# Windowed attention in layer 0: bias coefficients of 16 rows a head in 128x64 tiles, and the one-hot products in one turn

## The chip, the cores and the metric

The kernel runs on one core of a Trainium2 chip. The metric is the time of one execution on the device in microseconds (us), the median of several runs. A core has TensorE (PE in the profile; its weight loads are shown apart as PEld), VectorE (DVE), ScalarE (ACT), GpSimd (POOL) and SyncE (SP), which issues the transfers here. Matmul results land in PSUM[...]; VectorE and ScalarE carry them from there to SBUF.

## The reference

The input x is fp32, 2 images of 128 channels and 256x256 pixels. Two layers follow each other, both of the form x + f(groupnorm(x)). Layer 1 is a pair of convolutions whose product is added; the change doesn't touch it. Layer 0 is windowed attention with 4 heads of 32 channels: windows of 8x8 queries look at 12x12 keys around them.

```python
qkv = jnp.einsum('bchw,oc->bohw', x, W_qkv)
...
q = q * SCALE
attn = jnp.einsum('bnd,bmd->bnm', q, k)
attn = attn + rel_pos_emb(q, rel_height, rel_width) + FIXED_MASK
attn = jax.nn.softmax(attn, axis=-1)
out = jnp.einsum('bnm,bmd->bnd', attn, v)
...
return jnp.einsum('bchw,oc->bohw', out, W_out)
```

FIXED_MASK is minus infinity wherever the row distance or the column distance of query and key has the wrong parity. A query therefore meets only 6 key rows and 6 key columns, and a window falls into four classes by row parity and column parity, of 16 queries and 36 keys each. rel_pos_emb adds to each score one number for the key's column and one for its row; both are inner products of the query with a small table. For a query and a head there are thus 6 column coefficients and 6 row coefficients, from which the biases of all its keys are put together.

## The kernel before

An image is cut into 32 strips of 8 rows (strip k of 64 over both images). A strip is worked off in two units, u = 2k + r, one for each row parity r; both column parities c are handled inside the unit. Windows are taken in pairs side by side (e is 0 or 1), 16 pairs to a strip; the 8 pairs of one half of the strip share a PSUM bank for scores. A pair uses 60 keys in common, 10 columns j by 6 rows i, padded to 64; window e may see columns 4e to 4e + 5 only.

The scores of a unit stand in four banks, `sc[g][half]`: g is a pair of heads, half a half of the strip; column parity c picks partitions 0 to 63 or 64 to 127. Everything else that TensorE writes goes through one pool of four banks, `ps_pj`, handed out in turn: a new tile gets the bank of the fourth last, and must wait until that one has been read.

The biases are made in two steps:

- `coefficients(k, t2)` (L341). A query's place within its class is given by t2 (column, 0 to 3) and t1 (row, 0 to 3). For each of the 16 places, a matmul of the weights `wb[:, t2, t1]` (4 heads of 32 rows) with the gathered inputs `xq[:, t2, t1]` (4 classes a times 32 windows m, 128 columns) gives the coefficients of all queries in that place. The 32 rows of a head hold 6 column coefficients for window 0, the same 6 again for window 1, 6 row coefficients and 2 rows for flags. ScalarE (L358) writes the even windows into the tile `cf`, VectorE (L361) the odd ones; a scale and an addend of each row, `keep`, zero the rows of the other window and set a flag to 1.
- `biases(u, turn)` (L385). A matmul with a fixed one-hot matrix `hot` (32 rows by 64 keys for a head) spreads the coefficients over the keys, straight into the score banks; the flag rows bring the large negative number for keys that a window mustn't see. A turn is 8 matmuls of 32x64 with 256 columns. Turn 0 begins the banks, turn 1 fills in the other head of each pair; then `scores(u)` (L401) adds the products of keys and queries.

`by_place(k, columns)` (L292) gathers the normalised input into `xq` on GpSimd, two of the four t2 in each unit, for the strip after.

The order is written by hand for every engine (`manual_schedule`), so each engine runs its instructions in the order of the main loop (L493 to L526). In a unit u = 2k + r TensorE does: turn 1 of the biases, scores (L408), values (`f_pv`, L374), coefficients of the next strip for two t2 (`f_pa`, L352), attention outputs (`f_o`, L433), turn 0 of the biases of unit u + 1 (L393), its queries (`f_pq`, L330) and keys (`f_pk`, L309), and the output projection of u (`f_py`, L466). ScalarE takes exponentials (L417), half of the value copies (L380), coefficients, queries (L334) and keys (L310). VectorE takes the other value copies, coefficients, the division by the softmax sum (L439, L440), a transpose (L451), statistics (L111), the residual sum (L467) and the normalisation (L285).

Of the kernel before, what the change touches and what calls it, by code (L numbers as in the profile page):

```python
# [19 lines left out]
P = 128  # L20
# [28 lines left out]
def host_constants():  # L49
    ident = np.eye(P, dtype=np.float32)  # L50
    gavg = np.zeros((P, P), np.float32)
    for g in range(P // 4):
        gavg[4 * g : 4 * g + 4, 4 * g : 4 * g + 4] = 0.25

    kb = np.zeros((HEADS, 32, 6, 10), np.float32)
    for c in range(10):
        kb[:, c, :, c] = 1.0
    for r in range(6):
        kb[:, 10 + r, r, :] = 1.0
    kb[:, 16, :, 6:] = NEG  # L60
    kb[:, 17, :, :4] = NEG
    flag = np.zeros((2, 4 * NPAIR * 4, 2, 4), np.float32)
    flag[0, :, 0] = 1.0
    flag[1, :, 1] = 1.0


    hot = np.zeros((HEADS, 32, 64), np.float32)
    for key in range(64):
        j, i = divmod(key, 6)
        if key < 60:  # L70
            if j < 6:
                hot[:, j, key] = 1.0
            if j >= 4:
                hot[:, 6 + j - 4, key] = 1.0
            hot[:, 12 + i, key] = 1.0
        hot[:, 18, key] = 0.0 if j < 6 else NEG
        hot[:, 19, key] = 0.0 if 4 <= j < 10 else NEG

    keep = np.zeros((HEADS, 32, 2, 2), np.float32)
    for e in range(2):  # L80
        keep[:, 6 * e : 6 * e + 6, e, 0] = 1.0
        keep[:, 12:18, e, 0] = 1.0
        keep[:, 18 + e, e, 1] = 1.0

    sel = np.zeros((4, 32, P), np.float32)
    for ch in range(P):
        sel[:, ch % 8, ch] = 1.0
    return {
        "c_ident": ident,
        "c_sel": sel.reshape(P, P),  # L90
        "c_gavg": gavg,
        "c_kb": kb.reshape(P, 60),
        "c_flag": flag.reshape(2, 4 * NPAIR, 32),
        "c_hot": hot.reshape(P, 64),
        "c_keep": keep.reshape(P, 4),
        "c_head": np.stack([(np.arange(P) // DH % 2 == i) for i in range(2)], 1).astype(np.float32),
    }
# [47 lines left out]
def attention_fast(tc, io, x1_d, norm, st_x, st_y, tags, ends):  # L145
# [6 lines left out]
    with ExitStack() as l0:  # L152
# [8 lines left out]

        wqkvT = cload("wqkvT", io["w_qkvT"], [P, 3 * P])
        woT = cload("woT", io["w_outT"], [P, P])
        hot = cload("hot", io["c_hot"], [P, 64])
        keep = cload("keep", io["c_keep"], [P, 4])
        head = cload("head", io["c_head"], [P, 2])
        wq_s = cst.tile([P, P], F32, tag="f_wq_s", name="f_wq_s")
# [14 lines left out]
            for g in range(2)  # L182
        ]

        xq = cst.tile([P, 4, 4, 4, 2 * NPAIR], F32, tag="f_xq", name="f_xq")
        wb = cst.tile([P, 4, 4, HEADS, 32], F32, tag="f_wb", name="f_wb")
        for i in range(2):
            nc.gpsimd.memset(xn[i], 0.0)
            for r in range(2):
# [6 lines left out]
        with ExitStack() as setup:  # L196
            sp = setup.enter_context(tc.tile_pool(name="f_setup", bufs=6))


            wq_nat = sp.tile([P, P], F32, tag="wq_nat", name="f_wq_nat", bufs=1)  # L200
            nc.sync.dma_start(wq_nat, io["w_q"])
            relT = sp.tile([P, 2 * NREL], F32, tag="relT", name="f_relT", bufs=1)
            nc.sync.dma_start(relT, io["relT"])
            g_rel = sp.tile([P, HEADS, 2 * NREL], F32, tag="g_rel", name="f_g_rel", bufs=1)
            for h in range(HEADS):
                pg = ps_pj.tile([P, 512], F32, tag="pj", name=f"f_pg_{h}")


                for o in (0, NREL):
                    for m in (0, 64):  # L210
                        nc.tensor.matmul(
                            pg[m : m + 64, o : o + NREL], wq_nat[32 * h : 32 * h + 32, m : m + 64],
                            relT[32 * h : 32 * h + 32, o : o + NREL], start=True, stop=True,
                        )
                nc.scalar.mul(g_rel[:, h, :], pg[:, : 2 * NREL], SCALE)
            for t in range(4):
                o = 11 - 2 * t
                nc.scalar.copy(wb[:, t, 0, :, 0:6], g_rel[:, :, o : o + 11 : 2])
                nc.scalar.copy(wb[:, t, 0, :, 6:12], g_rel[:, :, o : o + 11 : 2])
                for t1 in range(1, 4):  # L220
                    nc.scalar.copy(wb[:, t, t1, :, 0:12], wb[:, t, 0, :, 0:12])
                o = NREL + 11 - 2 * t
                for t2 in range(4):
                    nc.scalar.copy(wb[:, t2, t, :, 12:18], g_rel[:, :, o : o + 11 : 2])
            for s in range(NS):
                t = sp.tile([P, 8, W], F32, tag="sx", name=f"f_sx_0_{s}")
                nc.sync.dma_start(t, x[0, :, 8 * s : 8 * s + 8, :])
                norm.chunk(st_x[0], 4 * s, t)
# [63 lines left out]
        def by_place(k, columns):  # L292
            cells = xn[k % 2].rearrange("p r c j i -> p (r c) j i")[:, :, 1:129, 1:5]
            for t2 in columns:
                nc.gpsimd.tensor_copy(xq[:, t2], cells.rearrange("p a (m b) i -> p b i a m", b=4)[:, t2])  # L295

        def old_keys(u):
            k, r = divmod(u, 2)
# [39 lines left out]

            return [lambda c=c: part(c) for c in range(2)]

        def coefficients(k, t2):  # L341

            if t2 == 0:
                cfs[k] = wk.tile([P, 4, NPAIR, 2, 4, 4], F32, tag="cf", name=f"f_cf_{k}")
            cf = cfs[k].rearrange("p a n e b t -> p e b t (a n)")
            bank = []

            def part(t1):
                if t1 == 0:
                    bank.append(ps_pj.tile([P, 512], F32, tag="pj", name=f"f_pa_{k}_{t2}"))  # L350
                pa = bank[0]
                nc.tensor.matmul(  # L352
                    pa[:, P * t1 : P * t1 + P], wb[:, t2, t1].rearrange("p h x -> p (h x)"),
                    xq[:, t2, t1].rearrange("p a m -> p (a m)"), start=True, stop=True,
                )
                if t1 == 3:
                    by_e = pa.rearrange("p (t m e) -> p e t m", t=4, e=2)
                    nc.scalar.activation(  # L358
                        cf[:, 0, t2], by_e[:, 0], AF.Identity, bias=keep[:, 1:2], scale=keep[:, 0:1]
                    )  # L360
                    nc.vector.tensor_scalar(  # L361
                        cf[:, 1, t2], by_e[:, 1], keep[:, 2:3], keep[:, 3:4], ALU.mult, ALU.add
                    )

            return [lambda t=t: part(t) for t in range(4)]

        def values(u, j):
            k, r = divmod(u, 2)
# [13 lines left out]
                    pv[rows].rearrange("p (n h d) -> p n h d", n=4, h=HEADS),  # L382
                )

        def biases(u, turn):  # L385

            k, r = divmod(u, 2)
            for i in range(2):
                half = (i + turn) % 2
                for h in (i, i + 2):  # L390
                    rows = slice(32 * h, 32 * h + 32)
                    for c in range(2):
                        nc.tensor.matmul(  # L393
                            sc[h // 2][half][64 * c : 64 * c + 64, :, i], hot[rows, :],
                            cfs[k][rows, 2 * r + c, 8 * half : 8 * half + 8].rearrange(
                                "p n e b t -> p n (e b t)"
                            ),
                            start=turn == 0, stop=False, skip_group_check=True,
                        )

        def scores(u):  # L401
            k, r = divmod(u, 2)
# [83 lines left out]
        with tc.manual_schedule(engines=ORDERED):  # L486
            normalise(0)
            by_place(0, range(4))
            for t2 in range(4):
                emit(coefficients(0, t2))  # L490
            biases(0, 0)
            emit(queries(0) + keys(0))
            for u in range(NU):  # L493
                k, r = divmod(u, 2)
                b, s = divmod(k, NS)
                later, more = u + 1 < NU, k + 1 < NB * NS
                if r == 0:
                    if k + 2 < NB * NS:
                        load_rows(k + 2)
                    if more:  # L500
                        normalise(k + 1)
                if u in stats_at:
                    input_stats(u)
                if more:
                    by_place(k + 1, (2 * r, 2 * r + 1))
                if later:
                    old_keys(u + 1)
                biases(u, 1)
                scores(u)
                for j in range(4):  # L510
                    values(u, j)
                if more:
                    emit(coefficients(k + 1, 2 * r) + coefficients(k + 1, 2 * r + 1))
                attend(u)
                turn(u)
                if later:

                    biases(u + 1, 0)
                    emit(queries(u + 1) + keys(u + 1))
                if u > 0:  # L520
                    result_stats(u - 1)
                project(u)
                if u in stats_at:
                    load_next()
                del qs[u]
# [819 lines left out]
```

## Time and profile before

| | |
|---|---|
| median of 3 runs | 3400.35 us (3399.28 to 3402.16) |
| span of the profiled run | 3402.5 us |
| layer 0, first to last coefficient matmul | 101.0 to 2182.8 us |
| granted TensorE clock | 0.991 |
| TensorE busy, 500 to 1000 us | 500.00 us |
| VectorE busy in it | 389.82 us |
| ScalarE busy in it | 288.05 us |
| GpSimd busy in it | 117.12 us |
| data moved | 104 GB/s over the span |

The groups of instructions that the change touches, with the count of records (a matmul leaves two), their busy time and the mean of one:

| line, engine | what | records | busy us | mean ns |
|---|---|---|---|---|
| L352 PE | coefficients, 128x128 with 128 columns | 2048 | 268.5 | 286 |
| L393 PE | one-hot products, 32x64 with 256 columns | 4096 | 176.4 | 400 |
| L358 ACT | coefficients to `cf`, 128x256 | 256 | 209.8 | 819 |
| L361 DVE | coefficients to `cf`, 128x256 | 256 | 196.0 | 765 |
| L295 POOL | gather into `xq`, 128x512 | 256 | 346.9 | 1386 |

Busy time of TensorE is a union: matmuls overlap, so a mean of 286 ns for a record says nothing of the rate. The rate is read from the chain or from a timeline, as the length of a stretch divided by its matmuls. A busy share alone doesn't say what sets the time either; for that one looks at which engine the chain of work lies on, and at whether that engine ever waits.

### The profile page before, as it was taken

To read this page: it belongs to the slowest core of one execution; us is meant where nothing else is said; L and a number is where in the kernel's file an instruction comes from. 1 tells how busy PE (TensorE), PEld (TensorE's weight loads), DVE (VectorE), ACT (ScalarE), POOL (GpSimd) and SP (SyncE) were. 2 spreads that over 40 slices of the span, in tenths; PEclk is the share of its full clock that TensorE was granted. 3 is DMA by queue.
4 is the path that set the end of the run, shared out by engine and by line. 5 is a ranking of instruction groups with operands and counts; after the bars stand their busy time and mean duration, and the time that the engine had idled before them with its cause. 6 is when DMAs were issued, how large, how long until landed. Compare 5 with 4: busy or idle time off the path is not lost.

```text
span 3402.5 us, 116586 instructions
## 1 busy us (share of the span) xinstructions
PE 3248.6 (95%) x52814; PEld 1977.8 (58%) x52814; DVE 2632.3 (77%) x3955; ACT 1602.4 (47%) x2675; POOL 940.0 (28%) x598
## 2 busy tenths in 40 slices
PE   0799999999999999999999999989999999999997
PEld 0567777777777777777777777733333333333333
DVE  8667777777777777767777676678888888888887
ACT  0455555555555555555555555523333323333332
POOL 2212122222222212122122221123333333333333
PEclk9999999999999999999999999989999999999999
DMA  9223233232332212222122221133333332333332
GB/s 397 104 102 117 90 123 114 93 117 97 116 117 86 92 65 80 71 81 80 65 80 79 73 80 65 53 103 124 122 112 113 124 124 99 121 112 114 124 124 83
DMA packets 115896, 360.28 MB, mean 106 GB/s; under 512 B 8128, under 2 KB 74304, under 8 KB 90816
## 3 DMA queue, kind: packets, MB, share of 16 engines
q1 hardware_dynamic: 115392, 352.72, 29.2%
q8 instruction: 419, 6.86, 0.8%
q14 instruction: 85, 0.70, 0.1%
HBM read 218.48 MB, written 134.22 MB: 104 GB/s over the span
## 4 chain that ended last, share of the span: by engine, by line
PE 95%; issue 2%; DVE 1%; DMA 1%; POOL 1%; ACT 0%; SPq 0%; POOLq 0%; DVEq 0%
PE a_p L636 26%; PE f_pv L374 14%; PE f_pa L352 8%; PE f_s L408 8%; PE f_o L433 7%; PE f_pq L330 7%; PE f_pk L309 7%; PE f_py L466 7%; PE g L622 5%; PE f_s L393 5%; PE b L706 2%; DMA f_sx<-in_x 0%; DVE t L695 0%; DMA raw<-f_x 0%; POOL f_kt L190 0%
## 5 line engine op out<-in xcount | busy, mean ns | idle before, releaser
L380 DVE COPY f_vt<-f_pv 64x512 f32<-64x512 f32 x512 | 355.0, 695 | 314.0 <-ACT f_vt L380 313.8
L636 PE MATMUL a_p<-xm,w 128*128 128x512 f32 (+1 forms) x1288 | 581.5, 597 | 0.0
L295 POOL COPY f_xq<-f_xn 128x512 f32<-128x512 f32 x256 | 346.9, 1386 | 846.2 <-DVE f_xn L285 846.2
L334 ACT ACTIVATE f_q<-f_pq,f_head 128x512 f32<-128x512 f32 x512 | 310.0, 688 | 362.0 <-PE f_pq L330 362.0
L374 PE MATMUL f_pv<-f_wqkvT,f_xn 128*64 128x128 f32 x8192 | 476.1, 274 | 0.0
L374 PEld LDWEIGHTS f_pv<-f_wqkvT,f_xn 128*64 128x64 f32 x8192 | 445.2, 137 | 8.7
L688 ACT ACTIVATE t<-t,w 128x1024 f32<-128x1024 f32 x128 | 147.3, 1151 | 619.9 <-DVE t L683 619.9
L636 PEld LDWEIGHTS a_p<-xm,w 128*128 128x128 f32 x1288 | 238.3, 189 | 331.4 <-issue 331.1
L695 DVE SCALAR_TENSOR_TENSOR t<-t,w,t 128x1024 f32<-128x1024 f32 x256 | 420.2, 1641 | 6.8 <-ACT t L688 1.7
L417 ACT ACTIVATE f_p<-f_s 128x512 f32<-128x512 f32 x512 | 264.3, 603 | 340.0 <-PE f_s L408 339.9
L380 ACT COPY f_vt<-f_pv 64x512 f32<-64x512 f32 x512 | 298.4, 583 | 111.7 <-PE f_pv L374 111.3
L723 POOL TENSOR_TENSOR y<-y,raw 128x768 f32<-128x768 f32 x62 | 169.2, 2729 | 541.5 <-DVE y L715 493.4
L724 POOL TENSOR_TENSOR y<-y,raw 128x1280 f32<-128x1280 f32 x64 | 246.3, 3848 | 164.3 <-DVE y L715 164.3
L278 POOL COPY f_xn<-f_xn 128x1048 f32<-128x1048 f32 x62 | 71.2, 1148 | 796.9 <-PE f_pv L374 796.9
L352 PE MATMUL f_pa<-f_xq,f_wb 128*128 128x128 f32 x2048 | 268.5, 286 | 17.1 <-DVE f_vt L380 11.2
L408 PEld LDWEIGHTS f_s<-f_q,f_kt 64*64 64x64 f32 x16384 | 252.2, 135 | 49.6 <-issue 49.6
L361 DVE TENSOR_SCALAR f_cf<-f_pa,f_keep 128x256 f32<-128x256 f32 x256 | 196.0, 765 | 100.3 <-ACT f_cf L358 100.2
L408 PE MATMUL f_s<-f_q,f_kt 64*64 64x64 f32 x16384 | 269.9, 220 | 0.0
L467 DVE TENSOR_TENSOR f_x<-f_py,f_raw 128x512 f32<-128x512 f32 x256 | 177.0, 692 | 119.7 <-PE f_py L466 119.7
L352 PEld LDWEIGHTS f_pa<-f_xq,f_wb 128*128 128x128 f32 x2048 | 244.2, 195 | 38.8 <-issue 25.7
L433 PE MATMUL f_o<-f_vt,f_p 128*32 128x66 f32 x16384 | 263.4, 222 | 0.0
L330 PE MATMUL f_pq<-f_xn,f_wq_s 128*128 128x512 f32 x512 | 255.4, 619 | 0.0
(117 smaller groups left out, 4458.8 us busy)
## 6 DMA issues: line engine op xcount, KB each, us to landing
f_raw<-in_x SPq DMA_DIRECT2D x62, 1280.0 KB, 8.1
f_sx<-in_x SPq DMA_DIRECT2D x64, 1024.0 KB, 7.7
f_x<-f_x SPq DMA_DIRECT2D x128, 512.0 KB, 3.4
out<-y SPq DMA_DIRECT2D x64, 1024.0 KB, 4.9
raw<-f_x SPq DMA_DIRECT2D x64, 640.0 KB, 6.4
raw<-f_x SPq DMA_DIRECT2D x62, 384.0 KB, 6.9
f_raw<-in_x SPq DMA_DIRECT2D x2, 1024.0 KB, 8.0
raw_pre<-f_x SPq DMA_DIRECT2D x2, 384.0 KB, 5.2
```

What stands on the lines that cost most here:

```text
L295: nc.gpsimd.tensor_copy(xq[:, t2], cells.rearrange("p a (m b) i -> p b i a m", b=4)[:, t2])
L330: nc.tensor.matmul(pq, wq_s, xn[k % 2][:, r, c, 1:129, 1:5], start=True, stop=True)
L334: nc.scalar.activation(q[:, c, :, i], pq.rearrange("p (n x) -> p n x", n=NPAIR), AF.Copy, scale=head[:, i : i + 1],)
L352: nc.tensor.matmul(pa[:, P * t1 : P * t1 + P], wb[:, t2, t1].rearrange("p h x -> p (h x)"), xq[:, t2, t1].rearrange("p a m -> p (a m)"), s ...
L374: nc.tensor.matmul(pv[64 * c : 64 * c + 64, P * n : P * n + P], xt[:, r, c, o : o + 64], wvT, start=True, stop=True,)
L380: (nc.vector.tensor_copy if c else nc.scalar.copy)(vt[rows, 4 * j : 4 * j + 4, :, c, 0:32], pv[rows].rearrange("p (n h d) -> p n h d", n=4 ...
L408: nc.tensor.matmul(sc[g][n // 8][64 * c : 64 * c + 64, n % 8].rearrange("p i x -> p (i x)"), keys_k[rows, c, 48 * n : 48 * n + 64], qs[u][ ...
L417: nc.scalar.activation(pts[u][:, g, 8 * half : 8 * half + 8].rearrange("p n i x -> p (n i x)"), sc[g][half].rearrange("p n i x -> p (n i x ...
L433: nc.tensor.matmul(po[32 * h : 32 * h + 32, n - lo], p[:, h // 2, n, h % 2], vt[:, n, h], start=True, stop=True,)
L636: nc.tensor.matmul(pa[:, : n * W], w, rows, start=i == 0, stop=i == len(terms) - 1)
L695: nc.vector.scalar_tensor_tensor(t3[:, j : j + 4], t1[:, j + tap : j + tap + 4, :], w3[:, tap : tap + 1], t3[:, j : j + 4], ALU.mult, ALU.add,
L724: nc.gpsimd.tensor_tensor(y[:, 3:8, :], y[:, 3:8, :], raws[b, s][:, 0:5, :], ALU.add)
```

## The change

Half of the rows in a coefficient matmul carried a second copy of the column coefficients, flags of the other window, or nothing. The change gives a head 16 rows: 6 column coefficients, 6 row coefficients, one flag, 3 unused. The weights of a place are then 128x64, and the two halves of a strip are computed beside each other in two column tiles of the array, 64 columns each: half 0 lands in partitions 0 to 63, half 1 in 64 to 127. One call makes the coefficients of two t2 into a single bank, and one ScalarE and one VectorE operation of 512 elements a partition empty it. What they tell apart is no longer the window e but the head i of a pair: each writes all columns and `keep` zeroes the rows of the other head.

The window is now told apart by the one-hot matrix, of which there are two (`hot[rows, e]`), with the flag's negative number in the columns that the window mustn't see. A block of 32 rows holds the two heads of a pair in one half, so the 16 one-hot products of a unit are still 16 matmuls of 32x64 with 256 columns. All are issued in one turn, right before the scores.

GpSimd's gathers are split by half: four of 256 elements a unit in place of two of 512. In the setup, the weights `wb` are laid out by other copies.

```diff
-    hot = np.zeros((HEADS, 32, 64), np.float32)
+    hot = np.zeros((2, HEADS, 16, 2, 64), np.float32)
...
+    keep = np.zeros((2, HEADS, 16, 2, 2), np.float32)
+    for i in range(2):
+        keep[:, i::2, 0:12, i, 0] = 1.0
+        keep[:, i::2, 12, i, 1] = 1.0
...
-        xq = cst.tile([P, 4, 4, 4, 2 * NPAIR], F32, tag="f_xq", name="f_xq")
-        wb = cst.tile([P, 4, 4, HEADS, 32], F32, tag="f_wb", name="f_wb")
+        xq = cst.tile([P, 4, 2, 4, 4, NPAIR], F32, tag="f_xq", name="f_xq")
+        wb = cst.tile([P, 4, 4, HEADS, 16], F32, tag="f_wb", name="f_wb")
...
             for t2 in columns:
-                nc.gpsimd.tensor_copy(xq[:, t2], cells.rearrange("p a (m b) i -> p b i a m", b=4)[:, t2])
+                for half in range(2):
+                    nc.gpsimd.tensor_copy(
+                        xq[:, t2, half],
+                        cells[:, :, 64 * half : 64 * half + 64].rearrange(
+                            "p a (m b) i -> p b i a m", b=4
+                        )[:, t2],
+                    )
...
-        def coefficients(k, t2):
...
+        def coefficients(k, r):
...
+            if r == 0:
+                cfs[k] = wk.tile([P, 2, 4, 8, 2, 16], F32, tag="cf", name=f"f_cf_{k}")
+            pa = ps_pj.tile([P, 512], F32, tag="pj", name=f"f_pa_{k}_{r}")
+            for t in range(8):
+                t2, t1 = 2 * r + t // 4, t % 4
+                for half in range(2):
+                    nc.tensor.matmul(
+                        pa[64 * half : 64 * half + 64, 64 * t : 64 * t + 64],
+                        wb[:, t2, t1].rearrange("p h x -> p (h x)"),
+                        xq[:, t2, half, t1].rearrange("p a m -> p (a m)"), start=True, stop=True,
+                    )
+            src = pa.rearrange("p (t m e) -> p e m t", t=8, e=2)
+            for i in range(2):
+                dst = cfs[k][:, :, :, :, i, 8 * r : 8 * r + 8].rearrange("p e a n t -> p e (a n) t")
+                if i == 0:
                     nc.scalar.activation(
-                        cf[:, 0, t2], by_e[:, 0], AF.Identity, bias=keep[:, 1:2], scale=keep[:, 0:1]
-                    )
+                        dst, src, AF.Identity, bias=keep[:, 1:2], scale=keep[:, 0:1]
+                    )
+                else:
                     nc.vector.tensor_scalar(
-                        cf[:, 1, t2], by_e[:, 1], keep[:, 2:3], keep[:, 3:4], ALU.mult, ALU.add
-                    )
+                        dst, src, keep[:, 2:3], keep[:, 3:4], ALU.mult, ALU.add
+                    )
...
-        def biases(u, turn):
+        def biases(u):
...
+            for e in range(2):
+                for half in range(2):
+                    for g in range(2):
+                        rows = slice(64 * half + 32 * g, 64 * half + 32 * g + 32)
+                        for c in range(2):
+                            nc.tensor.matmul(
+                                sc[g][half][64 * c : 64 * c + 64, :, :, 16 * e : 16 * e + 16].rearrange(
+                                    "p n i x -> p (n i) x"
+                                ),
+                                hot[rows, e],
+                                cfs[k][rows, e, 2 * r + c].rearrange("p n i x -> p (n i x)"),
+                                start=e == 0, stop=False, skip_group_check=True,
+                            )
...
-                biases(u, 1)
+                biases(u)
                 scores(u)
...
-                    emit(coefficients(k + 1, 2 * r) + coefficients(k + 1, 2 * r + 1))
+                    coefficients(k + 1, r)
                 attend(u)
                 turn(u)
                 if later:
-
-                    biases(u + 1, 0)
                     emit(queries(u + 1) + keys(u + 1))
```

More of the change, by code (lines that the diff above doesn't have):

```diff
@@ L64, in host_constants @@
     flag[1, :, 1] = 1.0
-    hot = np.zeros((HEADS, 32, 64), np.float32)
+    hot = np.zeros((2, HEADS, 16, 2, 64), np.float32)
     for key in range(64):
         j, i = divmod(key, 6)
[L70 to L83, printed above, removed]
+        for e in range(2):
+            if 0 <= j - 4 * e < 6:
+                hot[:, :, j - 4 * e, e, key] = 1.0
+            else:
+                hot[:, :, 12, e, key] = NEG
+            if key < 60:
+                hot[:, :, 6 + i, e, key] = 1.0
+    keep = np.zeros((2, HEADS, 16, 2, 2), np.float32)
+    for i in range(2):
+        keep[:, i::2, 0:12, i, 0] = 1.0
+        keep[:, i::2, 12, i, 1] = 1.0
     sel = np.zeros((4, 32, P), np.float32)
@@ L93, in host_constants @@
         "c_flag": flag.reshape(2, 4 * NPAIR, 32),
-        "c_hot": hot.reshape(P, 64),
+        "c_hot": hot.reshape(P, 128),
         "c_keep": keep.reshape(P, 4),
@@ L163, in attention_fast @@
         woT = cload("woT", io["w_outT"], [P, P])
-        hot = cload("hot", io["c_hot"], [P, 64])
+        hot = cload("hot", io["c_hot"], [P, 2, 64])
         keep = cload("keep", io["c_keep"], [P, 4])
@@ L217, in attention_fast @@
                 o = 11 - 2 * t
[L218 to L221, printed above, removed]
+                for t1 in range(4):
+                    nc.scalar.copy(wb[:, t, t1, :, 0:6], g_rel[:, :, o : o + 11 : 2])
                 o = NREL + 11 - 2 * t
                 for t2 in range(4):
-                    nc.scalar.copy(wb[:, t2, t, :, 12:18], g_rel[:, :, o : o + 11 : 2])
+                    nc.scalar.copy(wb[:, t2, t, :, 6:12], g_rel[:, :, o : o + 11 : 2])
             for s in range(NS):
@@ L339, in queries @@
             return [lambda c=c: part(c) for c in range(2)]
-        def coefficients(k, t2):
[L343 to L354, printed above, removed]
-                )
-                if t1 == 3:
-                    by_e = pa.rearrange("p (t m e) -> p e t m", t=4, e=2)
+        def coefficients(k, r):
[14 more added lines that the diff above has]
+                if i == 0:
                     nc.scalar.activation(
-                        cf[:, 0, t2], by_e[:, 0], AF.Identity, bias=keep[:, 1:2], scale=keep[:, 0:1]
+                        dst, src, AF.Identity, bias=keep[:, 1:2], scale=keep[:, 0:1]
                     )
+                else:
                     nc.vector.tensor_scalar(
-                        cf[:, 1, t2], by_e[:, 1], keep[:, 2:3], keep[:, 3:4], ALU.mult, ALU.add
+                        dst, src, keep[:, 2:3], keep[:, 3:4], ALU.mult, ALU.add
                     )
-            return [lambda t=t: part(t) for t in range(4)]
         def values(u, j):
@@ L383, in values @@
                 )
-        def biases(u, turn):
+        def biases(u):
             k, r = divmod(u, 2)
[L388 to L398, printed above, removed]
-                        )
+            for e in range(2):
+                for half in range(2):
[10 more added lines that the diff above has]
+                            )
         def scores(u):
@@ L488, in attention_fast @@
             by_place(0, range(4))
-            for t2 in range(4):
-                emit(coefficients(0, t2))
-            biases(0, 0)
+            coefficients(0, 0)
+            coefficients(0, 1)
             emit(queries(0) + keys(0))
```

## The prediction

> **What bounds the kernel now.** I read first the busy shares, then the chain of work that ended last.
>
> ```profile
> PE 3248.6 (95%) x52814; PEld 1977.8 (58%) x52814; DVE 2632.3 (77%) x3955; ACT 1602.4 (47%) x2675; POOL 940.0 (28%) x598
> ...
> PE 95%; issue 2%; DVE 1%; DMA 1%; POOL 1%; ACT 0%; SPq 0%; POOLq 0%; DVEq 0%
> ```
>
> TensorE is busy 95% of the span, and the chain lies on it for the same 95%: what it no longer has to do comes off the span, until another engine holds it up. The same chain in order of time, from 1000 to 1040 us, shows one unit of layer 0 (start, length, what; x counts records, two to a matmul):
>
> ```profile
> 1009.44 2.02 PE f_s L408 x128
> 1011.47 3.65 PE f_pv L374 x64
> 1015.11 1.98 PE f_pa L352 x16
> 1017.10 1.98 PE f_o L433 x128
> 1019.07 0.62 PE f_s L393 x16
> 1019.69 1.92 PE f_pq L330 x4
> 1021.61 1.75 PE f_pk L309 x4
> 1023.36 1.72 PE f_py L466 x4
> 1025.07 0.62 PE f_s L393 x16
> 1025.69 2.02 PE f_s L408 x128
> ```
>
> No gap: a unit is 2.02 + 3.65 + 1.98 + 1.98 + 0.62 + 1.92 + 1.75 + 1.72 + 0.62 = 16.26 us, and there are 128. The change touches 1.98 (coefficients) and 2 x 0.62 (one-hot products). What the other engines do with the coefficients is in the groups:
>
> ```profile
> L334 ACT ACTIVATE f_q<-f_pq,f_head 128x512 f32<-128x512 f32 x512 | 310.0, 688 | 362.0 <-PE f_pq L330 362.0
> L358 ACT ACTIVATE f_cf<-f_pa,f_keep 128x256 f32<-128x256 f32 x256 | 209.8, 819 | 91.8 <-PE f_pa L352 80.1
> L361 DVE TENSOR_SCALAR f_cf<-f_pa,f_keep 128x256 f32<-128x256 f32 x256 | 196.0, 765 | 100.3 <-ACT f_cf L358 100.2
> L467 DVE TENSOR_TENSOR f_x<-f_py,f_raw 128x512 f32<-128x512 f32 x256 | 177.0, 692 | 119.7 <-PE f_py L466 119.7
> ```
>
> The coefficient evacuations (L358, L361) handle half the elements of L334 and L467 and still take longer, and VectorE's starts when ScalarE's is done. The timelines of both engines give the order that will matter:
>
> ```profile
> 1016.24 1.77 ACT L358 ACTIVATE f_cf<-f_pa,f_keep 128x256 f32<-128x256 f32 x2 [0.44 <-PE f_pa L352]
> ...
> 1017.08 0.77 DVE L361 TENSOR_SCALAR f_cf<-f_pa,f_keep 128x256 f32<-128x256 f32 x1 [0.55 <-ACT f_cf L358]
> 1018.04 0.78 DVE L361 TENSOR_SCALAR f_cf<-f_pa,f_keep 128x256 f32<-128x256 f32 x1 [0.20 <-ACT f_cf L358]
> 1018.65 0.20 DVE L439 RECIPROCAL f_rc<-f_o 128x12 f32<-128x12 f32 x1
> ```
>
> ScalarE starts 0.14 us after the first bank is full (1015.04 + 1.06), VectorE 0.02 us after ScalarE ends, and the attention outputs queue behind on VectorE.
>
> [...] L433 puts 64 matmuls of 66 columns in four column tiles into 1.98 us, 124 ns for four, where a full-width matmul of L352 takes 1.98 / 8 = 248 ns for 128 columns. [...] L358 and L361 write each element 128 bytes from the last; L361 costs 765 ns for 256 elements where the 320 of L440 cost 492. [...] VectorE waits for ScalarE, 255 times here.
>
> **The change, part by part.**
>
> *Coefficient matmuls, on the path.* Per unit 8 matmuls of 128x128 with 128 columns become 16 of 128x64 with 64 columns, in pairs on two column tiles. A row of 64 columns with 64 weight columns is L408: 64 matmuls in four tiles in 2.02 us, 126 ns for four side by side; L433 (K = 128, as here) says 124. So 8 pairs x 126 = 1.01 us, and 1.98 - 1.01 = 0.97 us a unit come off. Bounds: L466 puts 2 x 512 columns through in 1.72 us, 1.68 ns each, so 8 x 64 x 1.68 = 0.86 us is the floor, and 1.12 off[...]. At the other end, no overlap within a pair: L374's 3.65 / 32 = 114 ns each, 1.82 us, 0.16 off. I take 0.97: L408 and L433 could not run at these rates if loads or tiles took turns.
>
> *One-hot products, on the path.* Still 16 matmuls of 32x64 with 256 columns a unit, but in one turn of 16. A turn of 8 is 0.62 us; its columns need 256 x 1.68 = 0.43, the other 0.19 is start and switch, paid twice now. One turn: 2 x 0.43 + 0.19 = 1.05, so 1.24 - 1.05 = 0.19 off; from 0 (each half pays its start) to 0.25. Nothing new is waited for: the coefficients are then half a unit old, the score banks emptied by the exponentials long before.
>
> *Evacuations, beside.* ScalarE and VectorE each have one of 512 elements instead of two of 256, now written in runs of 8 (32 bytes). With short runs no dearer than L334 and L467: 0.69 + 0.69 = 1.38 us, one after the other. If every element stayed as dear, an operation would cost twice the old one: 1.61 + 1.53 = 3.14. L310 writes runs of 4 at 624 ns, against 583 for L380, and L467 reads PSUM 16 bytes apart at no visible cost, so I take 0.70 + 0.75 = 1.45. The 256-byte steps in PSUM that the new reading makes stand in no row.
>
> *The bank of the coefficients, a wait to test.* A unit now takes 14 banks of the 4-bank pool instead of 15: 4 values, 1 coefficients, 3 outputs, 2 queries, 2 keys, 2 projections. The first query matmul reuses the bank of the coefficients, and behind it on TensorE stand all queries, keys and projections. On the old clock: values end at 1015.11, coefficients at 1016.1, ScalarE starts at 1016.24, VectorE ends at 1016.26 + 1.45 = 1017.71; TensorE wants the bank at 1015.11 + 1.01 + 1.98 = 1018.10. Spare 0.39 us, some 0.2 of it wanted for the weight load (188 ns). So free up to a sum of evacuations of about 1.65. The second query matmul needs the first output bank: VectorE takes 1018.65 to 1019.44 = 0.79 for it, so 1018.50 against 1019.06; keys and projection follow with more room.
>
> *Off the path.* Column gathers on GpSimd: four of 256 elements for two of 512 (2.71 us a pair, from 1012.07). With 0.2 of fixed cost (L300: 673 ns for 524, L278: 1148 for 1048) each is 0.79, the second placement ready at 1015.25; TensorE wants it at 1008.83 + 1.05 + 2.02 + 3.65 + 0.5 = 1016.05. Hidden. VectorE sheds about 0.78 us a unit, ScalarE 0.94. One-time parts: the four opening coefficient groups (6.63 us now) and gathers, some 2 us less and 1 more; left out. Layer 1 is the same.
>
> Sum: 0.97 + 0.19 = 1.16 us, x 128 = 148 us. 3400.35 - 148 = **3252**.
>
> **The rivals.**
>
> *Evacuations dearer in part.* Sum of the two about 2.1: VectorE frees the bank at 1018.36, and with the weight load TensorE starts some 0.45 late. 1.16 - 0.45 = 0.71, x 128 = 91: **3309**. For: the unseen reading step, and L358 at 819. Against: L467, L310.
>
> *Strided cost in full.* Sum 3.14: bank free at 1019.40 against 1018.10, 1.3 late, plus 0.2 for weights: 1.5 - 1.16 = 0.34 lost a unit, 44 us: **3444**, slower. For: if reading, not writing, made L358 and L361 dear, nothing got better. Against: L467 reads apart in the same bank kind and pays nothing.
>
> *No overlap of the two halves.* 0.16 + 0.19 = 0.35, x 128 = 45: **3355**. For: weight loads of L374, 137 ns mean, fill its 3.65 us just as well as its columns do. Against: L408 and L433.
>
> A VectorE bound is no rival: (2632.3 - 128 x 0.78) of 3252 is 78%.
>
> **How the numbers follow.** Forecast 0.76; evacuations dearer in part 0.12; no overlap 0.07; full strided cost 0.05. Within the forecast, 1.12 + 0.25 = 1.37 off gives 3225 and 0.80 + 0 gives 3298. The range goes from 3225 to 3312, which takes in the first rival and leaves 0.12 out. Slower is the full strided cost, 0.05; of the rest I leave 0.01 to no change, so faster is 0.94.
>
> **What would show it.** Coefficients at about 1.0 us and one-hot products at about 1.05 us of the chain per unit, a unit of 15.1 us; the ScalarE and VectorE coefficient groups near 0.70 and 0.75; no wait of the query matmuls for the coefficient evacuation. Wrong: groups at 1.2 us or more with TensorE waiting there every unit, or a coefficient stretch of 1.8.

## The result, and the profile after

The changed kernel takes 3428.62 us (median of 4 runs, 3425.88 to 3436.59) against 3401.1 us for the kernel before on the same chip: a ratio of 1.0085, with an interval of 1.0068 to 1.0103. It is slower by 27.5 us, where 148 us less were forecast.

The page of the changed kernel, first the engines, then the instruction queue and the chain:

```profile
PE 3150.4 (92%) x54862; PEld 1911.4 (56%) x54862; DVE 2551.8 (74%) x3827; ACT 1498.2 (44%) x2543; POOL 950.2 (28%) x854
...
q8 instruction: 434, 7.11, 0.8%
...
PE 91%; issue 6%; DVE 1%; POOL 1%; DMA 1%; ACT 0%; SPq 0%; POOLq 0%; DVEq 0%
```

TensorE is busy for 98 us less than before (3248.6 - 3150.4), and the span is longer all the same. No other engine has taken its place in the chain: "issue" has, from 2% to 6%. That is time in which TensorE waited for nothing that the profile shows. The chain in order of time shows where it lies (start, length, what, records):

```profile
1008.55 1.64 PE f_pv L380 x26
1010.19 0.06 PE f_pa L356
1010.24 0.05 PE f_pv L380
1010.30 0.93 PE f_pa L356 x30
1011.23 1.16 PE f_o L440 x69
1012.39 1.88 issue
1014.26 1.11 PE f_o L440 x59
1015.38 1.92 PE f_pq L333 x4
1017.29 1.76 PE f_pk L312 x4
1019.05 1.72 PE f_py L473 x4
1020.77 1.05 PE f_s L399 x32
1021.82 2.02 PE f_s L415 x128
1023.84 1.46 PE f_pv L380 x22
1025.30 1.36 issue
```

The stretches of work are as forecast: 1.05 us for the one-hot products, about 1.0 for the coefficients, 2.02 for the scores. But TensorE stops for 1.88 us in the middle of the attention outputs, between two matmuls of one bank, and for 1.36 us in the middle of the values. The last copy of values before the first of these pauses ended at 1011.69 us, so no operand was missing. The counts point to the reason. An earlier pause ends at 1008.55; from there to the next are 26 + 1 + 1 + 30 + 69 = 127 records, and from that one to the third 59 + 4 + 4 + 4 + 32 + 128 + 22 = 253. Those are 128 and twice 128, but for a few records missing from the trace. A record of a matmul has a weight load beside it, so 128 records are 256 instructions. The queue line names the same amount: 7.11 MB in 434 packets is 16.4 KB each, and twice 54862 instructions over 434 packets is 253 in each, 255 with the semaphore instructions of TensorE's queue. Such a packet is called a block below, of 256 instructions by the distance of the pauses. That distance is one block or two, so the pauses are read as falling where a new block of instructions begins. The trace shows the blocks come in: packets of the instruction queue land at 1007.04, 1012.94 and 1025.16 us, and TensorE goes on at 1008.55, 1014.26 and 1026.66, each time 1.3 to 1.5 us after a landing.

All of layer 0 was counted in this way, from the starts of TensorE's instructions in the trace (loads, multiplications and the semaphore instructions of its queue). At the 399 places where the count modulo 256 is 193, the time from one start to the next adds up to 172 us; at another position it is some 8 us (the median over the 256). The difference, 164 us, is lost at block edges. In the kernel before no idle time over 0.1 us on TensorE falls there. Forecast and result are 175 us apart (148 + 27.5); the block edges hold 164 of them.

The rest lies behind the longest pauses. The granted clock of the profiled run is 0.987, where it was 0.991. The clock records of the trace show TensorE at half clock in 14 stretches, 89 us in all; in the kernel before there are 7, 65 us in all. Here is one (start, length, what, records):

```profile
842.83 2.72 issue
845.55 0.81 PE f_o L440 x32
846.37 3.41 PE f_pq L333 x4
```

The query matmuls take 3.41 us where they took 1.92 above; the clock was at half from 845.9 to 849.4 us. Of the 12 steps of 2.7 us or more at block edges in layer 0, 8 are followed by such a stretch within 5 us, of the shorter ones none, and the kernel before has no such step there. That the long pauses bring the half clock about is read from this order in time; no run separates the two. The 24 us more at half clock cost 12 us at half rate, which is what the block edges leave of the 175, within 1 us.

The evacuations of the coefficients, from the timelines of ScalarE and VectorE:

```profile
1030.24 0.78 ACT L365 ACTIVATE f_cf<-f_pa,f_keep 128x512 f32<-128x512 f32 x1 [0.29 <-PE f_pa L356]
...
1031.06 0.81 DVE L369 TENSOR_SCALAR f_cf<-f_pa,f_keep 128x512 f32<-128x512 f32 x1 [0.38 <-ACT f_cf L365]
```

They take 0.78 + 0.81 = 1.59 us, within the 1.65 that the prediction called free, and the waits of TensorE name no coefficient evacuation.

### The profile page after: what moved, and what is told of

Read it like the earlier page. It is cut to its first block, busy times and chain, and to the rows that moved or that the text cites. A ratio compares the mean times of both kernels' runs of the same rounds, so it can differ in the third digit from the quotient of the medians.

```text
span 3428.1 us, 120552 instructions
## 1 busy us (share of the span) xinstructions
PE 3150.4 (92%) x54862; PEld 1911.4 (56%) x54862; DVE 2551.8 (74%) x3827; ACT 1498.2 (44%) x2543; POOL 950.2 (28%) x854
## 3 DMA queue, kind: packets, MB, share of 16 engines
q8 instruction: 434, 7.11, 0.8%
## 4 chain that ended last, share of the span: by engine, by line
PE 91%; issue 6%; DVE 1%; POOL 1%; DMA 1%; ACT 0%; SPq 0%; POOLq 0%; DVEq 0%
PE a_p L640 26%; PE f_pv L380 14%; PE f_o L440 8%; PE f_s L415 8%; PE f_pq L333 7%; PE f_pk L312 7%; PE f_py L473 6%; PE g L626 5%; PE f_s L399 4%; PE f_pa L356 4%; PE b L710 2%; DMA f_sx<-in_x 0%; DVE t L699 0%; POOL f_xq L293 0%; POOL f_kt L189 0%
## 5 line engine op out<-in xcount | busy, mean ns | idle before, releaser
L293 POOL COPY f_xq<-f_xn 128x256 f32<-128x256 f32 x512 | 358.0, 746 | 760.3 <-DVE f_xn L282 760.3
L380 PE MATMUL f_pv<-f_wqkvT,f_xn 128*64 128x128 f32 x8192 | 493.4, 275 | 19.1 <-issue 18.3
L380 PEld LDWEIGHTS f_pv<-f_wqkvT,f_xn 128*64 128x64 f32 x8192 | 452.2, 137 | 38.0 <-issue 28.9
L440 PE MATMUL f_o<-f_vt,f_p 128*32 128x66 f32 x16384 | 290.7, 224 | 96.7 <-issue 93.3
L440 PEld LDWEIGHTS f_o<-f_vt,f_p 128*32 128x32 f32 x16384 | 254.6, 111 | 118.5 <-issue 105.9
L333 PE MATMUL f_pq<-f_xn,f_wq_s 128*128 128x512 f32 x512 | 265.6, 641 | 1.3 <-DVE f_on L447 1.3
L312 PE MATMUL f_pk<-f_xn,f_wqkvT 128*128 128x512 f32 x512 | 248.0, 605 | 0.0
L473 PE MATMUL f_py<-f_ot,f_woT 128*128 128x512 f32 x512 | 240.3, 591 | 1.7 <-DVE f_ot L458 1.7
```

Of the source, the lines that this page charges most:

```text
L293: nc.gpsimd.tensor_copy(xq[:, t2, half], cells[:, :, 64 * half : 64 * half + 64].rearrange("p a (m b) i -> p b i a m", b=4)[:, t2],)
L312: nc.tensor.matmul(pk, wkT, xt[:, r, c, 1:129, 2:6], start=True, stop=True)
L333: nc.tensor.matmul(pq, wq_s, xn[k % 2][:, r, c, 1:129, 1:5], start=True, stop=True)
L380: nc.tensor.matmul(pv[64 * c : 64 * c + 64, P * n : P * n + P], xt[:, r, c, o : o + 64], wvT, start=True, stop=True,)
L440: nc.tensor.matmul(po[32 * h : 32 * h + 32, n - lo], p[:, h // 2, n, h % 2], vt[:, n, h], start=True, stop=True,)
L473: nc.tensor.matmul(py, woT, ots.pop((u, c)), start=True, stop=True)
```

## The experiments

**Theory A**: TensorE starves for instructions; blocks of 256 come one at a time (in the traces their transfers start at least 3.2 us apart and take at most 1.7), and the changed order uses some of them up faster than the next arrives. **Theory B**: a hidden wait for data or for a bank. **Theory C**: issuing all one-hot products in one turn is what costs. The times of the kernel before beside these runs were 3400.06 to 3401.54 us.

### Fewer instructions for the same columns

```diff
-                    for h in range(HEADS):
+                    for g in range(2):
                         nc.tensor.matmul(
-                            po[32 * h : 32 * h + 32, n - lo], p[:, h // 2, n, h % 2],
-                            vt[:, n, h], start=True, stop=True,
+                            po[64 * g : 64 * g + 64, n - lo],
+                            p[:, g, n].rearrange("p i x -> p (i x)"),
+                            vt[:, n, 2 * g], start=True, stop=True,
```

> The changed kernel, with the attention outputs of a head pair in one matmul of 128x64 instead of two of 128x32: 32 matmuls a unit for 64, in two column tiles instead of four, with 66 columns each as before, so the same 1.98 us of columns. (The second head of a pair gets the values of the first, so this leaves part of the attention out.) Theory A, TensorE starves for instructions: its stream arrives in blocks of 256 instructions, one at a time, and the stretch of coefficients, outputs and what follows uses them up faster than they come. A matmul here is four instructions (two loads, two multiplications), so a unit has 664 instead of 792: pauses of about 163 us in all shrink to below 30, time 3270 to 3300 us. Theory B, a hidden wait for data or for a bank (values not yet evacuated, the bank of the coefficients): nothing of that changes, 3428 us within 15.

> The same edit in the kernel before: 632 instead of 760 instructions a unit. Theory A: the kernel before hardly starves, so fewer instructions bring nothing: 3390 to 3402 us. If wide outputs are simply faster on TensorE, this falls as much as the changed kernel does, by 100 us or more. Theory B: 3401.

Measured: 3299.63 us for the changed kernel (ratio to the kernel before 0.9699, 0.9683 to 0.9716) and 3412.59 for the kernel before (1.0037, 1.0023 to 1.0051). The edit takes 129 us off one and adds 13 to the other. The 3412.59 lies above the 3390 to 3402 of theory A, the 3299.63 within its range. In the kernel before, wide outputs are thus no faster in themselves; what they save is instructions, 128 a unit, and only the changed kernel was short of them. A small part of the 129 is work: in the chain of the changed kernel the outputs take 1.87 us where they took 1.98 (their tile shape is now that of the coefficients ahead; a change of shape is read as 0.17 us in a run below), 14 us in 128 units. At the block edges 78 us are left of 172. TensorE's waits from 112 to 2150 us (engine, line, cause: us in all, times, longest), in the changed kernel:

```profile
PE f_o L440 <- issue: 88.7, 75, 3.3
```

and with wide outputs:

```profile
PE f_o L440 <- issue: 17.1, 16, 1.9
```

Over all lines of layer 0 the waits that are called issue fall from 118 us (88.7 + 17.5 + 7.7 + 4.1) to 47 (17.1 + 21.0 + 5.4 + 2.3 + 1.3); theory A left less than 30. Theory B, by which nothing should have changed, falls.

### More instructions for the same columns

In the kernel before, each output matmul of 66 columns is split into two of 33.

```diff
-                    for h in range(HEADS):
+                    for c in range(2):
+                        for h in range(HEADS):
...
-                            po[32 * h : 32 * h + 32, n - lo], p[:, h // 2, n, h % 2],
-                            vt[:, n, h], start=True, stop=True,
+                                po[32 * h : 32 * h + 32, n - lo, c], p[:, h // 2, n, h % 2],
+                                vt[:, n, h, c], start=True, stop=True,
```

> The kernel before, with each attention output matmul of 66 columns split into two of 33: the same columns and results, 128 matmuls a unit for 64, 1016 instructions for 760. TensorE itself should need some 2.2 us for them instead of 1.98, 33 us in all. Theory A: the stream of instructions becomes the bound also in this kernel; the model says pauses of 440 to 520 us: 3700 to 3970 us, with pauses that no other engine explains. If only the work on TensorE counts: 3420 to 3450.

Measured: 3850.08 us (1.1306, 1.1282 to 1.1331). The pauses can be made in the kernel that had none, by more instructions for the same columns. Of the 195 pauses over 0.25 us in its layer 0 (112 to 2672 us), 190 lie where the count modulo 256 is 193 or 194, as in the changed kernel. In the chain:

```profile
1015.34 1.45 PE f_o L434 x134
1016.79 2.29 issue
```

The 2.2 us expected for the work of the outputs was the author's estimate: at the pace of these 134 records, 256 take some 2.8. Not all of the 449 us more is pause: half clock fills 216 us of this run, where it filled 65.

### The turn alone

`biases(u, e)` is called for e = 0 after the attention outputs and for e = 1 before the scores.

```diff
-        def biases(u):
+        def biases(u, e):
...
+            biases(0, 0)
...
-                biases(u)
+                biases(u, 1)
                 scores(u)
...
                 if later:
+                    biases(u + 1, 0)
                     emit(queries(u + 1) + keys(u + 1))
```

> The changed kernel, with the one-hot products of window 0 back in the old place, right after the attention outputs, and those of window 1 before the scores: as many instructions, two turns. Theory A: TensorE works 0.19 us a unit longer, 24 us, and the pauses stay about as they are, since outputs are now followed by 64 more instructions at a high rate: 3428 + 24, 3435 to 3465 us. Theory C, issuing all products in one turn is what costs: the loss of the turn comes back, 3330 us or less.

Measured: 3491.73 us (1.0265, 1.0248 to 1.0282), 63 us above the changed kernel and more than theory A gave. Theory C falls: the turn is a gain. The forecast 0.19 us a unit accounts for 24 us of the 63; the pauses that the waits show grow from 118 to 133 us (101.6 + 12.2 + 10.5 + 6.8 + 2.1), 15 more. The other 24 are the clock: the granted clock fell to 0.980, and the 140 us at half clock are 51 more than in the changed kernel, 25 us at half rate. This run is also the coefficient part by itself, with the turns as they were: the part that was to bring most makes the kernel 92 us slower.

### Another order

The same instructions, with stretches of few instructions (queries, keys and projection use 24 in 5.4 us) between the dense ones:

```diff
+            biases(0)
...
-                biases(u)
                 scores(u)
...
+                q = queries(u + 1) if later else []
+                emit(q[:1])
                 if more:
                     coefficients(k + 1, r)
+                emit(q[1:])
                 attend(u)
                 turn(u)
                 if later:
-                    emit(queries(u + 1) + keys(u + 1))
+                    emit(keys(u + 1))
+                    biases(u + 1)
```

> The changed kernel with the same instructions in another order: after the values, the first query matmul, coefficients, the second query matmul, attention outputs, keys, one-hot products of the next unit, projection. Slow stretches (512 columns from 4 instructions) now lie between the fast ones. Theory A: in a model with blocks of 256 and 5 us from asking for a block to using it, pauses fall from 140 to 59 us; so about 90 us less, 3310 to 3365. Theory B: evacuations have as much time as before, 3428 within 20.

Measured: 3364.34 us (0.9892, 0.9876 to 0.9909), faster than both kernels. The outputs' pauses fall from 88.7 to 19.1 us. The order has its price:

```profile
1008.81 1.06 PE f_pq L333 x2
1009.87 1.08 PE f_pa L356 x32
1010.95 1.06 PE f_pq L333 x2
...
1013.98 1.95 PE f_pk L312 x4
...
1016.98 1.91 PE f_py L473 x4
```

Query, key, coefficient and projection stretches take 2.12, 1.95, 1.08 and 1.91 us here, where 1.92, 1.76, 0.99 and 1.72 stand in the chain above: 0.67 us a unit for four more changes of tile shape, 0.17 us each.

A second order has both query matmuls ahead of the coefficients:

```diff
+            biases(0)
...
-                biases(u)
                 scores(u)
...
+                if later:
+                    emit(queries(u + 1))
                 if more:
                     coefficients(k + 1, r)
                 attend(u)
                 turn(u)
                 if later:
-                    emit(queries(u + 1) + keys(u + 1))
+                    emit(keys(u + 1))
+                    biases(u + 1)
```

> As the spread order, but both query matmuls together ahead of the coefficients: values, queries, coefficients, outputs, keys, one-hot products of the next unit, projection, scores. Two changes of tile shape fewer in a unit; in the trace of the spread order each query matmul took 1.06 us instead of 0.96. Theory A: pauses stay small (the model says 55 to 58 us for 59 and 50), and a unit loses about 0.2 us: 3364 - 25, 3325 to 3360 us. Theory that the spread order gained by moving the query matmuls between coefficients and outputs only for the sake of their evacuation: no change from 3364 or worse.

Measured: 3394.54 us (0.9983, 0.9976 to 0.999), a miss. Its chain leaves TensorE for another reason:

```profile
1004.05 2.42 ACT f_q L337 x4
1006.47 0.68 ACT f_cf L365
1007.15 0.03 issue
1007.18 0.82 DVE f_cf L369
1008.00 0.04 issue
1008.04 2.02 PE f_pk L312 x4
```

Four query evacuations, 2.42 us, now stand ahead of the coefficients' one in ScalarE's order, and the key matmuls reuse the bank of the coefficients. This is the wait that the prediction feared, in an order that it did not speak of. A third order moves the queries between coefficients and outputs, so that the coefficients' evacuation comes first:

```diff
                 if more:
                     coefficients(k + 1, r)
+                if later:
+                    emit(queries(u + 1))
                 attend(u)
                 turn(u)
                 if later:
-                    emit(queries(u + 1) + keys(u + 1))
+                    emit(keys(u + 1))
```

> The changed kernel with one move: the queries of the next unit between the coefficients and the attention outputs, everything else in the old order. The fast stretch of 160 records (coefficients and outputs) is cut in two by 1.9 us in which TensorE needs only 16 instructions, at the price of about one more change of tile shape (0.15 to 0.2 us a unit). The coefficients' evacuation stays ahead of the queries' on ScalarE, which the queries-first order got wrong: there the key matmuls waited for it in the chain. Theory A: pauses about halved, 3345 to 3385 us, like the spread order. Theory B: 3428 within 20.

Measured: 3353.4 us (0.9859, 0.9843 to 0.9876). One move of two matmuls (8 instructions, not the 16 of the expectation) turns the loss into a gain.

### What delays the blocks

> The changed kernel, with the input rows of the first four strips used again for all later ones, and one block of input statistics used throughout: the 2.3 MB that are loaded per strip in the first image (1.3 in the second) are left out, the results are stored as before. Nothing changes on any compute engine. Theory A with contention (a block of instructions waits behind the data transfers): in the trace of the changed kernel a transfer of instructions starts some 1.3 to 1.5 us after it can be asked for when no data move, and 2.4 to 4.5 us when they do, so most pauses go: 3290 to 3350 us. Theory A with a fixed delay: the pauses stay, 3428 within 15. Theory B (hidden wait among the engines): 3428 within 15.

```diff
+            if k >= 4:
+                raws[k] = kept[k % 4]
+                return
...
-            raws[k] = t
+            raws[k] = kept[k] = t
...
+                if "sx" in kept:
+                    sxs[u] = kept["sx"]
+                    return
```

Measured: 3320.32 us (0.9758, 0.9742 to 0.9774), 108 us less without a change on any compute engine. Counted as above, the block edges hold 96 us where they held 172, and of the outputs' 88.7 us of waits this is left:

```profile
PE f_o L446 <- issue: 30.8, 58, 1.2
```

So the transfers of data delay the instruction blocks. They don't do so alone: pauses remain without the loads. Instead of leaving loads out, they can be set apart:

```diff
-                if r == 0:
-                    if k + 2 < NB * NS:
-                        load_rows(k + 2)
+                if r == 1 and k + 2 < NB * NS:
+                    load_rows(k + 2)
+                if r == 0:
                     if more:
```

> The changed kernel, with the input rows of a strip asked for in the other unit of the strip (16 us before), so that they no longer follow directly on the load for the statistics: same bytes, two bursts instead of one. Theory A with contention: delays become shorter but more frequent; a gain of 0 to 40 us, 3388 to 3428. Theory A with a fixed delay, or theory B: 3428 within 15.

Measured: 3392.1 us (0.9972, 0.9962 to 0.9983), 37 us less for the same bytes. The edit asks for the rows one unit later, not earlier, so rows that come earlier can't be the reason. The block edges hold 150 us instead of 172, and half clock fills 59 us instead of 89. Both remedies together, in the two good orders:

> The same order, with the loads apart as well. Theory A with contention: both remedies act on the same pauses, so their gains add up in part only: 10 to 30 us below the same order without, 3320 to 3365 us. If the loads apart helped for another reason (earlier input rows), the full 36 us come on top.

> The spread order with the loads apart. The trace of the spread order has only some 19 us of pauses without a cause among the engines left; theory A says that no more than these can go: 3345 to 3364 us. If the loads apart helped for another reason, the full 36 us: 3328.

Measured: 3348.8 us (0.9846, 0.9829 to 0.9862) and 3346.88 us (0.9839, 0.9823 to 0.9856). Loads apart bring 5 us (10 to 30 were expected) and 17 us here where they brought 37, so they act on the same pauses. In the waits of the spread order with the loads apart, this is what is left for the outputs:

```profile
PE f_o L440 <- issue: 2.3, 4, 1.5
```

The spread order with the loads apart is 55 us below the kernel before. It and the other order are within each other's interval; no kernel with the full computation that ran was faster.

## Why the prediction was wrong

- **Coefficient matmuls, 0.97 us a unit: right.** The stretch went from 1.98 to 0.99 us (0.06 + 0.93 in the chain); in the kernel without loads it reads 0.93. The rival without overlap of the two halves is out.
- **One-hot products, 0.19 us: right.** One turn is 1.05 us, as worked out.
- **Evacuations, 1.45 us: measured 1.59.** VectorE's was 0.06 and ScalarE's 0.08 longer than taken; that includes whatever the large steps in PSUM cost. No stall followed, as said, so both rivals on evacuation are out.
- **Gathers, 0.79 us each: measured 0.746**, hidden but for 6 us in 5 waits over the whole kernel.
- **The step that failed: "what it no longer has to do comes off the span, until another engine holds it up".** There was a further holder, TensorE's own instruction stream. The prediction counted columns and never instructions. Here a coefficient matmul of 128 columns became two of 64, side by side, in half the time (1.98 to 0.99 us a unit) with twice the instructions (32 to 64): a unit goes from 760 to 792, and coefficients plus outputs from 288 instructions in 3.96 us to 320 in 3.0. The coefficients ahead of the outputs, 32 instructions in 1.98 us before, left time for a block to arrive; they are now 64 in 0.99. This cost 164 us at block edges and 12 us at half clock, against 148 saved. None of the rivals had it. The one that came nearest to the measured time, full strided cost at 3444, was wrong in its mechanism.
- A line of the page before would have given a warning, that of the instruction queue:

```profile
q8 instruction: 419, 6.86, 0.8%
```

At 0.8% of the transfer engines it looks like nothing. The share is no measure here: one packet is under way at a time (the starts are at least 3.2 us apart, a transfer takes at most 1.7), and what counts by theory A is how long one takes from asking to use.

One rival to the count of instructions was not run: where the block edges fall. With the semaphore instructions of TensorE's queue a unit of the kernel before has 768 instructions, three blocks exactly, so its edges stay at the same places in nearly every unit, and the run with more instructions has 1024, four blocks; the changed kernel's 799 move on from unit to unit. A third of the edges of the kernel before lie in the outputs too (127 of 381), without a pause. But no run moved them, so it isn't shown that this kernel would be free of pauses wherever they fell.

That a block is asked for when the stream enters the block before it is inferred from the starts of the transfers, at which at most 296 instructions were left; no run varied the size of a block or the number in hand. The moment of asking is in no trace, so the times from asking in the expectations (1.3 to 1.5 us, 2.4 to 4.5, and the 5 us of the model) are the author's estimates.

## What to carry to other kernels

Before cutting a matmul into smaller ones side by side, count TensorE's instructions as well as its columns, for each stretch of 256: coefficients and outputs went without a pause at 288 instructions in 3.96 us here, and had pauses at 320 in 3.0. An idle TensorE with cause "issue" in the middle of a run of like matmuls, at one or two times 128 records from the last (127 and 253 in the chain above), pointed to this wait here. It was shortened by long matmuls placed between short ones (the outputs' pauses from 88.7 to 19.1 us), by fewer and larger instructions (172 to 78 us at block edges), and by moving data bursts away (172 to 150). Each change of tile shape that an order adds has a price that must be set against it, 0.17 us here.

## What the runs showed of the hardware

In the traces of both kernels, transfers of instructions start at least 3.2 us apart, and start when at most 296 instructions are still to be worked off: that is about one block in hand, not more. The transfer of a block takes 0.88 to 1.7 us, and in the changed kernel a block that lands when the stream has run dry is used 1.2 to 1.6 us later. In the kernel before, never fewer than 15 instructions were left when a block landed; in the changed one, 40 of some 390 landed at 5 or fewer. These are counted from the starts and lengths of the instruction queue's transfers, set against the starts of TensorE's instructions. The kernel before, at 256 instructions in 5.4 us on average (16.26 us for 768), had no pause over 0.1 us at a block edge; the changed kernel lost 164 us there, and the run with 1016 instructions for matmuls a unit had 190 pauses over 0.25 us there. Written in runs of 8 elements, and read from PSUM in larger steps, the coefficients' evacuation went from 819 ns for 256 elements to 778 for 512 on ScalarE, and from 765 to 810 on VectorE.
